# A four-layer graph network on one core: the adjacency loaded once, ScalarE's order in the first stage written by the program, and layer 0's mixing back moved behind the next group's first weight

## The chip, the cores and the metric

The kernel runs on one core of a Trainium2 chip. The metric is the device time of one execution in microseconds (us), the median of several runs. The profile is one more execution, with its own span.

The names used here: TensorE or PE for the matrix engine, VectorE or DVE, ScalarE or ACT, GpSimd or POOL, SyncE or SP. SyncE and ScalarE each have a queue on which the program issues transfers (DMA).

## The reference

The input x has 128 batches of 64 nodes with 256 features; adj is one 64 x 64 matrix for all batches. Four layers follow each other, and each ends in a residual and a layer norm: x = layernorm(x + f(x)).

- Layer 0 is three graph convolutions, relu after the first two: h = relu((adj * adj) (x W1)), with widths 256 to 512, 512 to 1024, 1024 to 256. The weighting is adj * adj elementwise.
- Layer 1 takes the eigenvectors U of the normalized Laplacian of adj, and computes U (relu((U^T x) W1 + b1) W2 + b2).
- Layer 2 is two graph convolutions with adj, then four small LSTMs over windows of 1 to 4 nodes.
- Layer 3 is an attention masked and scaled by adj.

The eigenvectors are computed on the chip too, by Householder steps, bisection and a recurrence, on 64 x 64 tiles. They need adj alone, and layer 1 needs them.

## The kernel before, in words

**Tiling.** The 8192 rows (128 batches x 64 nodes) are 64 tiles of 128 rows; each tile holds two batches, so that a 64 x 64 matrix acts on a tile as a 128 x 128 block-diagonal matrix. All of x stays in one tile X of the on-chip memory. Four tiles (512 rows) are a group; there are 16 groups.

**Two stages.** The first stage runs layer 0 for all groups, and beside it the eigenvectors. The second stage runs layers 1 to 3, three groups at a time. The diff touches the first stage and the loads ahead of it.

**Layer 0 of a group** (`layer0`, line 747). `mixed` multiplies by sqT2, the block-diagonal transpose of adj * adj: it writes transposed products of a block of columns into PSUM, and ScalarE copies them out (m1 from X, m2 from h1). Then come the first weight aw1 (four pairs of 128 x 512 matmuls, each followed by a ScalarE relu into h1, helper `relu`, line 728), the second mixing of h1, the second weight aw2 and the third, aw3. The second weight is done by a Strassen-like scheme: 14 products per group, VectorE sums (ss, tw, the joins into h2), a ScalarE relu of each joined quarter. After the third weight ScalarE copies the result to s3. The mixing back (lines 855 to 862) multiplies s3 by sqT2, two tiles at a time, VectorE adds the result to X, and the layer norm (`scalar_norm`, line 567) is put on the list `norms`: per two tiles two sums, two sums of squares and two final scalings on ScalarE, with a root on GpSimd (lines 578 to 580) between.

**Order.** Two groups are in flight. A loop at the end of the stage (lines 873 to 889) plays the groups as Python generators against a model clock `now`: each matmul adds its cost to it, and a yield says when the group may go on. `between`, called after each matmul, lets the eigenvector generator `eigen` go on when its own time has come; that generator keeps the modelled time at which VectorE is free (`free`) and yields `soon()` or `full(turns)`, a little before or after it. A norm is taken off the list at each of the 14 products (line 835). What is issued in this loop keeps the order of issue on the engines named in `manual_schedule` (line 869): before, TensorE and VectorE. ScalarE's instructions are put in order by the compiler's scheduler, from priorities and its own estimate of times.

**Start.** The adjacency is loaded five times: twice into the diagonal blocks of the zeroed ad2 and once into a64, on ScalarE's queue, and late on SyncE's queue twice into adst, a stack of two copies. The first work of TensorE is the transpose of ad2 (line 871), from which VectorE makes adT2 and sqT2; only then can the first group be mixed. The eigenvectors start from a64 (line 104): degrees, a square root on ScalarE (line 117), scaling matrix dm, and the product with dm on TensorE (line 133), for which the program leaves room with `full(1)`. Each Householder step then has a ScalarE square root (line 174) and one product pc, for which ScalarE writes a half of LV (line 165).

Of the kernel before, what the change touches and what calls it, by code (L numbers as in the profile page):

```python
# [10 lines left out]
F32 = mybir.dt.float32  # L11
AF = mybir.ActivationFunctionType
ALU = mybir.AluOpType
AX = mybir.AxisListType

N = 64
# [39 lines left out]
def eigen(tc, stack, a, ident, cst, u2, ut2, now, free):  # L56
# [9 lines left out]
    nc = tc.nc  # L66
    until = [0.0]
    V, S, PE = Timed(nc.vector, free, until), nc.scalar, nc.tensor
# [5 lines left out]
    def sb(shape, tag):  # L74
        uid[0] += 1
        return wp.tile(shape, F32, tag=tag, name=f"{tag}_{uid[0]}")
# [9 lines left out]
    def soon():  # L86
        return max(free[0], until[0]) - 0.45

    def full(turns=0):
        return max(free[0], until[0]) + 0.3 + 0.6 * turns  # L90
# [23 lines left out]
    dg = sb([N, 1], "c3")  # L114
    V.tensor_scalar(dg, deg, 1e-30, None, op0=ALU.max)
    y = sb([N, 1], "c4")
    S.activation(y, dg, AF.Sqrt)
    V.reciprocal(y, y)
    for _ in range(2):
# [9 lines left out]
    dm = sb([N, N], "dm")  # L129
    V.tensor_scalar(dm, C["eye"], y, None, op0=ALU.mult)  # L130
    pm = ps([N, N], "pa")
    yield full(1)
    mm(pm, m, dm)


# [26 lines left out]
    for i in range(N - 2):  # L162
        j = i + 1
        L = LV[j % 2]
        S.copy(L[:N, 1, :], eye[:, j:j + 1].to_broadcast([N, N]))
        q = sb([N, 16], "q")
        rest, ss, sq, g0, sg, rc, n2, vv, th, s0, c2, qi = (q[:, k:k + 1] for k in range(12))
        u = sb([N, 8], "u")
        v, av, vt, pt, qt = (u[:, k:k + 1] for k in range(5))
        v0 = xr[:, j:j + 1]  # L170
        V.scalar_tensor_tensor(sb([N, N + 1], "junk")[:, j + 1:], xr[:, j + 1:], 1.0, xr[:, j + 1:], op0=ALU.mult,
                               op1=ALU.mult, accum_out=rest)
        V.tensor_scalar(ss, v0, v0, rest, op0=ALU.mult, op1=ALU.add)
        S.activation(sq, ss, AF.Sqrt)
        root = free[0] + 0.6
        yield soon()
        for update in late:
            update()
            yield soon()
        V.tensor_scalar(g0, rest, 1.5e-30, -1.0, op0=ALU.is_gt, op1=ALU.mult)  # L180
        V.tensor_scalar(sg, v0, 0.0, 0.5, op0=ALU.is_ge, op1=ALU.subtract)
        until[0] = root
        yield soon()
        V.reciprocal(rc, sq)
        V.tensor_scalar(n2, ss, rc, sq, op0=ALU.mult, op1=ALU.add)
        V.scalar_tensor_tensor(v0, n2, sg, v0, op0=ALU.mult, op1=ALU.add)
        yield soon()
        V.scalar_tensor_tensor(sb([N, N + 1], "junk")[:, j:N], xr[:, j:N], 1.0, eye[:, j:], op0=ALU.mult,
                               op1=ALU.mult, accum_out=v)
        V.tensor_copy(L[:N, 0, :], v.to_broadcast([N, N]))  # L190
        yield full()
        pq = ps([W, 2, N], "pc")
        mm(pq, L, AQ)
        there, until[0] = until[0], 0.0
        V.tensor_scalar(vv, v0, v0, rest, op0=ALU.mult, op1=ALU.add)
        V.reciprocal(vv, vv)
        V.tensor_mul(th, vv, g0)
        yield soon()
        V.tensor_scalar(s0, v0, th, 2.0, op0=ALU.mult, op1=ALU.mult)
        V.scalar_tensor_tensor(sb([N, N + 1], "junk")[:, j:N], A[:, j:], 1.0, xr[:, j:N], op0=ALU.mult,  # L200
                               op1=ALU.mult, accum_out=av)
        V.tensor_scalar(u[:, 2:4], u[:, 0:2], th, 2.0, op0=ALU.mult, op1=ALU.mult)
        until[0] = there
        yield soon()
        V.scalar_tensor_tensor(sb([N, N + 1], "junk")[:, j:N], pq[:N, 0, j:], th, xr[:, j:N], op0=ALU.mult,
                               op1=ALU.mult, accum_out=c2)
        qr = sb([N, N], "qr")
        V.scalar_tensor_tensor(qr[:, j:], xr[:, j:N], c2, pq[:N, 0, j:], op0=ALU.mult, op1=ALU.add)
        yield soon()
        V.tensor_scalar(qi, qr[:, j:j + 1], th, 2.0, op0=ALU.mult, op1=ALU.mult)  # L210
        nx = xrs[j % 2]
        V.scalar_tensor_tensor(nx[:, j + 1:N], qr[:, j + 1:], s0, pq[N:, 0, j + 1:], op0=ALU.mult, op1=ALU.add)
        V.scalar_tensor_tensor(nx[:, j + 1:N], xr[:, j + 1:N], qi, nx[:, j + 1:N], op0=ALU.mult, op1=ALU.add)
        yield soon()


        def update_a(qt=qt, vt=vt, c2=c2, pt=pt, qr=qr, xr=xr, j=j):
            V.scalar_tensor_tensor(qt, vt, c2, pt, op0=ALU.mult, op1=ALU.add)
            V.scalar_tensor_tensor(A[:, j:], qr[:, j:], vt, A[:, j:], op0=ALU.mult, op1=ALU.add)
            V.scalar_tensor_tensor(A[:, j:], xr[:, j:N], qt, A[:, j:], op0=ALU.mult, op1=ALU.add)  # L220

        def update_q(pq=pq, vt=vt):
            V.scalar_tensor_tensor(QT, pq[:N, 1, :], vt, QT, op0=ALU.mult, op1=ALU.add)

        late = [update_a, update_q]
        xr = nx
# [5 lines left out]
    d, e, ep, g = (de[:, j:j + 1] for j in range(4))  # L232
# [31 lines left out]
    nrm, s1, s1s, s2e, hs = co_[1:6]  # L264
# [18 lines left out]
    lo, h, top, tgt, at, to = co_[14:20]  # L283
# [232 lines left out]
    pt = ps([N, N], "pa")  # L516
# [16 lines left out]
P = 128  # L533
# [62 lines left out]
def kernel(  # L596
# [25 lines left out]
    nc = tc.nc  # L622
    V, S, PE = nc.vector, nc.scalar, nc.tensor
    NT = ROWS // P
    x_t = x.rearrange("b n f -> (b n) f").rearrange("(t p) f -> p t f", p=P)
# [7 lines left out]
    keep = ctx.enter_context(tc.tile_pool(name="keep", bufs=1))  # L633
# [3 lines left out]
    phase_a = ctx.enter_context(ExitStack())  # L637
    wa = phase_a.enter_context(tc.tile_pool(name="wa", bufs=1))
    pa = phase_a.enter_context(tc.tile_pool(name="pa", bufs=1))
    ea = phase_a.enter_context(tc.tile_pool(name="ea", bufs=1))  # L640
# [5 lines left out]
        return t  # L646

    X = keep.tile([P, NT, D], F32, name="X")
    ad2 = keep.tile([P, P], F32, name="ad2")
    nc.gpsimd.memset(ad2, 0.0)  # L650
    adst = keep.tile([P, N], F32, name="adst")
    a64 = ea.tile([N, N], F32, name="a64")
    eig_c = ea.tile([P, len(CONSTS), N], F32, name="eig_c")
    for h in range(2):
        hs = slice(h * N, (h + 1) * N)
        nc.scalar.dma_start(ad2[hs, hs], adj)
    nc.scalar.dma_start(a64, adj)
    for t in range(2):
        nc.sync.dma_start(X[:, t, :], x_t[:, t, :])
    aw1 = load(wa, "aw1", a_w1, "(k p) f -> p k f", [P, 2, 512], p=P)  # L660
    nc.sync.dma_start(X[:, 2:4, :], x_t[:, 2:4, :])
    aw2 = wa.tile([P, 4, 1024], F32, name="aw2")
    for h in range(2):
        cols = slice(h * 512, (h + 1) * 512)
# [2 lines left out]
    for t in range(4, NT, 2):  # L667
        nc.sync.dma_start(X[:, t:t + 2, :], x_t[:, t:t + 2, :])
    nc.sync.dma_start(eig_c, consts)
    for h in range(2):  # L670
        nc.sync.dma_start(adst[h * N:(h + 1) * N, :], adj)

    ident = keep.tile([P, P], F32, name="ident")
    make_identity(nc, ident)
# [1 line left out]
    nc.gpsimd.memset(half, -0.5)  # L676
    ones = keep.tile([P, P], F32, name="ones")
    nc.gpsimd.memset(ones, 1.0)
    adT2 = keep.tile([P, P], F32, name="adT2")
    sqT2 = keep.tile([P, P], F32, name="sqT2")  # L680
    rs_row = keep.tile([P, P], F32, name="rs_row")
    rs_col = keep.tile([P, 1], F32, name="rs_col")
    u2 = keep.tile([P, P], F32, name="u2")
    ut2 = keep.tile([P, P], F32, name="ut2")
# [19 lines left out]
    now = [0.0]  # L704
# [42 lines left out]
    def layer0(g):  # L747
# [97 lines left out]
        for t in (2, 0):  # L845
# [6 lines left out]
                        done["third"] = g  # L852
                    yield now[0]
            S.copy(s3[:, t:t + 2, :], p)
        yield now[0] + 1.5
        for t in (2, 0):
            p = tl(psa, [P, 2, D], "ps", bufs=6)
            mm(p, sqT2, s3[:, t:t + 2, :])
            yield now[0] + 0.4
            x2 = xs[:, t:t + 2, :]  # L860
            VL.tensor_add(x2, p, x2)
            norms.extend(scalar_norm(tc, small, x2, half, spare))

    todo = [layer0(g) for g in range(NT // 4)]
    eig.extend([0.0, eigen(tc, phase_a, a64, ident, eig_c, u2, ut2, now, free)])
    going = []
    with tc.manual_schedule(engines={mybir.EngineType.PE, mybir.EngineType.DVE}):
        pt = tl(psa, [P, 512], "ps", bufs=6)  # L870
        PE.transpose(pt[:, :P], ad2, ident)
        V.tensor_copy(adT2, pt[:, :P])
        V.tensor_mul(sqT2, adT2, adT2)
        while todo or going or eig:
            while todo and len(going) < 2:
                going.append([0.0, todo.pop(0)])
            able = [x for x in going if x[0] <= now[0] + 0.05]
            if able:
                pick = able[0]
            else:  # L880
                pick = min(going + ([eig] if eig else []), key=lambda x: x[0])
                now[0] = max(now[0], pick[0])
            between()
            if pick is eig:
                continue
            try:
                pick[0] = next(pick[1])
            except StopIteration:
                going.remove(pick)
# [1 line left out]
    pr = tl(psa, [P, 512], "ps", bufs=6)  # L891
    PE.matmul(pr[:, :P], ones, adT2, start=True, stop=True)
    V.tensor_copy(rs_row, pr[:, :P])
    V.tensor_reduce(rs_col, ad2, AX.X, ALU.add)
    V.tensor_scalar(wide["c_b0"], wide["c_b0"], rs_col, None, op0=ALU.mult)
    V.tensor_add(cbi, cbi, cbh)
    phase_a.close()
# [354 lines left out]
```

## Time and profile before

| | before |
|---|---|
| median of 3 runs | 2570.01 us |
| lowest, highest | 2565.66, 2570.18 us |
| span of the profiled execution | 2566.4 us |
| its mean granted clock of TensorE | 0.994 of full |
| first mixing by sqT2 starts | 8.0 us |
| first stage ends (first product by u2, layer 1) | 876 us |

How to read the views: the page gives the busy time of each engine, in which matmuls that wait in the array's pipeline count as busy. The view of waits says who waited for whom, in all, how often, and the longest. A row of the timeline is: start, length, engine, line, operation, output <- inputs, shape, count, and in brackets the idle time before it and what ended it. "L51" is a recording helper through which all of the eigenvector code's VectorE work goes; "L719" is that of nearly all matmuls. One matmul of the program is two instructions in the profile (32-bit data).

### The profile page before, as it was taken

How to read it: one execution, taken by the hardware profiler on the slowest of the kernel's cores; microseconds unless marked ns; L12 is line 12 of the kernel's file. 1: busy time of each engine (PE TensorE's matmuls, PEld its weight loads, DVE VectorE, ACT ScalarE, POOL GpSimd, SP SyncE). 2: the span in 40 equal slices, each digit the busy share in tenths (PEclk: the TensorE clock that was granted, in tenths of full speed). 3: DMA queues.
4: the chain of work that ended last, by engine and by line, in shares of the span. 5: the costliest groups of instructions: out<-in, count | busy, mean ns of one | idle time of the engine just before them, and what ended most of it. 6: DMA issues, size and time to landing. Idle time of an engine off the chain costs nothing.

```text
span 2566.4 us, 39034 instructions
## 1 busy us (share of the span) xinstructions
PE 2502.8 (98%) x15020; PEld 2193.7 (85%) x15020; DVE 1414.7 (55%) x5001; ACT 1120.2 (44%) x2727; POOL 133.3 (5%) x316
## 2 busy tenths in 40 slices
PE   8999999999999999999999999999999999999996
PEld 7788887888877889889989889899898898978995
DVE  6877777778884433444453544534435445353235
ACT  3343333433333344544444454444444545445444
POOL 0000000000000100000000000000000000000001
PEclk9999999999999999999999999999999999999998
DMA  6000000000000300000000000000000000000000
GB/s 218 1 1 1 1 1 1 1 1 1 1 1 1 115 1 1 9 9 1 9 6 4 9 1 9 9 1 9 4 6 9 1 9 9 1 9 1 1 1 25
DMA packets 24811, 32.15 MB, mean 13 GB/s; under 512 B 2352, under 2 KB 21552, under 8 KB 24624
## 3 DMA queue, kind: packets, MB, share of 16 engines
q1 hardware_dynamic: 24384, 29.60, 3.4%
q8 instruction: 118, 1.93, 0.3%
q14 instruction: 69, 0.57, 0.1%
q10 hardware_dynamic: 240, 0.05, 0.0%
HBM read 21.25 MB, written 8.39 MB: 12 GB/s over the span
## 4 chain that ended last, share of the span: by engine, by line
PE 81%; DVE 10%; ACT 5%; POOL 2%; issue 1%; DMA 0%; ACTq 0%; POOLq 0%; DVEq 0%
PE ps L719 78%; POOL ln_rs L553 1%; DVE br L51 1%; DVE Q L51 1%; DVE X L563 1%; PE ps L924 1%; ACT gates L1027 1%; DVE ln_st L550 1%; DVE h L51 1%; PE ps L1140 1%; DVE D L51 1%; ACT spare L575 1%; ACT L1027 1%; ACT L1153 1%; DVE X L1090 1%
## 5 line engine op out<-in xcount | busy, mean ns | idle before, releaser
L719 PE MATMUL ps<-w,wih 128*128 128x128 f32 (+2 forms) x4992 | 895.1, 319 | 1.7 <-DVE w L1046 1.7
L719 PEld LDWEIGHTS ps<-w,wih 128*128 128x128 f32 x4992 | 764.5, 191 | 50.9 <-issue 8.4
L1027 ACT ACTIVATE gates<-ps,cbi 128x128 f32<-128x128 f32 (+2 forms) x1248 | 501.7, 409 | 581.9 <-PE ps L719 577.1
L719 PE MATMUL ps<-hs,whh 128*128 128x128 f32 (+2 forms) x3072 | 542.1, 303 | 4.4 <-DVE hs L1037 4.3
L719 PEld LDWEIGHTS ps<-hs,whh 128*128 128x128 f32 x3072 | 453.8, 191 | 33.8 <-issue 11.0
L1032 DVE TENSOR_TENSOR gates<-gates 128x128 f32<-128x128 f32 (+2 forms) x256 | 89.5, 350 | 253.9 <-ACT gates L1027 253.8
L719 PE MATMUL ps<-aw,h 128*128 128x256 f32 x1024 | 227.4, 379 | 0.1
L719 PEld LDWEIGHTS ps<-aw,h 128*128 128x128 f32 x1024 | 192.9, 190 | 26.7 <-ACT h L728 1.2
L728 ACT ACTIVATE h<-h 128x512 f32<-128x512 f32 x128 | 80.8, 631 | 240.3 <-DVE h L51 240.3
L1035 ACT ACTIVATE gates<-c 128x128 f32<-128x128 f32 (+2 forms) x288 | 98.3, 341 | 109.8 <-DVE c L1034 104.0
L1031 DVE TENSOR_TENSOR c<-c,gates 128x128 f32<-128x128 f32 (+2 forms) x192 | 62.5, 325 | 107.7 <-ACT gates L1027 105.3
L719 PE MATMUL ps<-aw,m 128*128 128x512 f32 x256 | 120.9, 593 | 0.0
L719 PE MATMUL ps<-ss,aw 128*128 128x256 f32 x512 | 118.0, 380 | 0.0
L719 PE MATMUL ps<-ss,tw 128*128 128x256 f32 x512 | 118.0, 380 | 0.0
L719 PE MATMUL ps<-m,aw 128*128 128x256 f32 x512 | 117.1, 379 | 0.0
L1046 DVE TENSOR_TENSOR w<-gates 128x256 f32<-128x256 f32 (+2 forms) x160 | 59.4, 377 | 102.3 <-PE ps L719 62.9
L1037 DVE TENSOR_TENSOR hs<-gates 128x128 f32<-128x128 f32 (+2 forms) x192 | 62.8, 328 | 92.6 <-ACT gates L1035 52.8
L563 DVE TENSOR_SCALAR X<-X,ln_mv,ln_rs 128x256 f32<-128x256 f32 x184 | 68.1, 411 | 82.2 <-POOL ln_rs L553 82.2
L719 PEld LDWEIGHTS ps<-m,aw 128*128 128x128 f32 x512 | 96.5, 190 | 18.9 <-issue 5.3
L719 PEld LDWEIGHTS ps<-ss,tw 128*128 128x128 f32 x512 | 96.2, 190 | 13.7 <-issue 1.0
L719 PEld LDWEIGHTS ps<-ss,aw 128*128 128x128 f32 x512 | 96.3, 190 | 12.8
L552 POOL TENSOR_SCALAR ln_rs<-ln_mv 128x2 f32<-128x2 f32 x96 | 23.1, 241 | 1573.0 <-DVE ln_mv L551 1571.2
(294 smaller groups left out, 3142.4 us busy)
## 6 DMA issues: line engine op xcount, KB each, us to landing
out_dram<-X SPq DMA_DIRECT2D x32, 256.0 KB, 2.1
X<-in_x_dram SPq DMA_DIRECT2D x31, 256.0 KB, 6.0
wih<-in_c_ih_dram SPq DMA_DIRECT2D x4, 1024.0 KB, 7.2
aw<-in_a_w_dram SPq DMA_DIRECT2D x3, 1024.0 KB, 9.6
whh<-in_c_hh_dram SPq DMA_DIRECT2D x3, 1024.0 KB, 9.3
aw<-in_a_w_dram SPq DMA_DIRECT2D x1, 512.0 KB, 4.9
cw<-in_c_w_dram SPq DMA_DIRECT2D x2, 256.0 KB, 3.6
X<-in_x_dram SPq DMA_DIRECT2D x2, 128.0 KB, 2.2
```

What stands on the lines that cost most here:

```text
L51: return getattr(self.engine, name)(out, *args, **kw)
L550: nc.vector.bn_stats(st[:, t, :], x[:, t, :])
L553: nc.gpsimd.tensor_tensor(rs, rs, half[:, :n], ALU.pow)
L563: nc.vector.tensor_scalar(x[:, t, :], x[:, t, :], mv[:, t, 0:1], rs[:, t:t + 1], op0=ALU.subtract, op1=ALU.mult)
L719: PE.matmul(out, lhsT, rhs, start=start, stop=stop)
L728: S.activation(dst, src, AF.Relu)
L1027: S.activation(gate[q][:, h, :], pp, AF.Tanh if q == "g" else AF.Sigmoid, bias=bias[:, j:j + 1])
L1031: V.tensor_mul(c[:, h, :], c[:, h, :], gate["f"][:, h, :])
L1032: V.tensor_mul(to, gate["i"][:, h, :], gate["g"][:, h, :])
L1035: S.activation(gate["i"][:, h, :], c[:, h, :] if p > 1 else to, AF.Tanh)
L1037: V.tensor_mul(new[:, h, :], gate["o"][:, h, :], gate["i"][:, h, :])
L1046: V.tensor_mul(hT[:, h, slice(first + p - 1, first + nw * p, p), :], gate["o"][:, h, :].rearrange("p (w b) -> p w b", b=8), gate["i"][:, h ...
```

## The change

The diff does four things.

1. The adjacency comes in once, stacked in adst, one half on each queue ahead of everything else; X[:, 2:4] goes to ScalarE's queue. ad2 and a64 are gone: the transpose reads adst and gives 64 x 128, from which two copies fill the diagonal blocks of adT2 (zeroed by GpSimd), and the eigenvectors read the upper half of adst. The purpose is to have the first data sooner.
2. A square root of a constant at the start asks for ScalarE's table before the first data, and `full(4)` leaves more layer-0 matmuls ahead of the product with dm.
3. ScalarE's order in the first stage is now the order of issue, as TensorE's and VectorE's. So that a square root isn't issued too early, a `yield soon()` goes ahead of it in two places.
4. The mixing back waits 6.5 us of the model clock, not 1.5, in all groups but the last. In the built program this puts it behind the next group's four first-weight pairs; before, the two mixings back stood between these pairs. The second mixing of the next group follows it, and in most groups half of the first mixing of the group after stands ahead of that and half behind.

```diff
@@ -114,6 +114,7 @@
     dg = sb([N, 1], "c3")
     V.tensor_scalar(dg, deg, 1e-30, None, op0=ALU.max)
     y = sb([N, 1], "c4")
+    yield soon()
     S.activation(y, dg, AF.Sqrt)
     V.reciprocal(y, y)
     for _ in range(2):
@@ -129,7 +130,7 @@
     dm = sb([N, N], "dm")
     V.tensor_scalar(dm, C["eye"], y, None, op0=ALU.mult)
     pm = ps([N, N], "pa")
-    yield full(1)
+    yield full(4)
     mm(pm, m, dm)
 
 
@@ -171,9 +172,9 @@
         V.scalar_tensor_tensor(sb([N, N + 1], "junk")[:, j + 1:], xr[:, j + 1:], 1.0, xr[:, j + 1:], op0=ALU.mult,
                                op1=ALU.mult, accum_out=rest)
         V.tensor_scalar(ss, v0, v0, rest, op0=ALU.mult, op1=ALU.add)
+        yield soon()
         S.activation(sq, ss, AF.Sqrt)
         root = free[0] + 0.6
-        yield soon()
         for update in late:
             update()
             yield soon()
@@ -646,19 +647,14 @@
         return t
 
     X = keep.tile([P, NT, D], F32, name="X")
-    ad2 = keep.tile([P, P], F32, name="ad2")
-    nc.gpsimd.memset(ad2, 0.0)
     adst = keep.tile([P, N], F32, name="adst")
-    a64 = ea.tile([N, N], F32, name="a64")
     eig_c = ea.tile([P, len(CONSTS), N], F32, name="eig_c")
-    for h in range(2):
-        hs = slice(h * N, (h + 1) * N)
-        nc.scalar.dma_start(ad2[hs, hs], adj)
-    nc.scalar.dma_start(a64, adj)
+    nc.scalar.dma_start(adst[:N, :], adj)
+    nc.sync.dma_start(adst[N:, :], adj)
+    nc.scalar.dma_start(X[:, 2:4, :], x_t[:, 2:4, :])
     for t in range(2):
         nc.sync.dma_start(X[:, t, :], x_t[:, t, :])
     aw1 = load(wa, "aw1", a_w1, "(k p) f -> p k f", [P, 2, 512], p=P)
-    nc.sync.dma_start(X[:, 2:4, :], x_t[:, 2:4, :])
     aw2 = wa.tile([P, 4, 1024], F32, name="aw2")
     for h in range(2):
         cols = slice(h * 512, (h + 1) * 512)
@@ -667,8 +663,6 @@
     for t in range(4, NT, 2):
         nc.sync.dma_start(X[:, t:t + 2, :], x_t[:, t:t + 2, :])
     nc.sync.dma_start(eig_c, consts)
-    for h in range(2):
-        nc.sync.dma_start(adst[h * N:(h + 1) * N, :], adj)
 
     ident = keep.tile([P, P], F32, name="ident")
     make_identity(nc, ident)
@@ -676,7 +670,10 @@
     nc.gpsimd.memset(half, -0.5)
     ones = keep.tile([P, P], F32, name="ones")
     nc.gpsimd.memset(ones, 1.0)
+
+    S.activation(keep.tile([P, 1], F32, name="root"), ones[:, 0:1], AF.Sqrt)
     adT2 = keep.tile([P, P], F32, name="adT2")
+    nc.gpsimd.memset(adT2, 0.0)
     sqT2 = keep.tile([P, P], F32, name="sqT2")
     rs_row = keep.tile([P, P], F32, name="rs_row")
     rs_col = keep.tile([P, 1], F32, name="rs_col")
@@ -852,11 +849,12 @@
                         done["third"] = g
                     yield now[0]
             S.copy(s3[:, t:t + 2, :], p)
-        yield now[0] + 1.5
+
+        yield now[0] + (1.5 if g == NT // 4 - 1 else 6.5)
         for t in (2, 0):
             p = tl(psa, [P, 2, D], "ps", bufs=6)
             mm(p, sqT2, s3[:, t:t + 2, :])
-            yield now[0] + 0.4
+            yield now[0]
             x2 = xs[:, t:t + 2, :]
             VL.tensor_add(x2, p, x2)
             norms.extend(scalar_norm(tc, small, x2, half, spare))
@@ -864,12 +862,14 @@
 
 
     todo = [layer0(g) for g in range(NT // 4)]
-    eig.extend([0.0, eigen(tc, phase_a, a64, ident, eig_c, u2, ut2, now, free)])
+    eig.extend([0.0, eigen(tc, phase_a, adst[:N, :], ident, eig_c, u2, ut2, now, free)])
     going = []
-    with tc.manual_schedule(engines={mybir.EngineType.PE, mybir.EngineType.DVE}):
+    with tc.manual_schedule(engines={mybir.EngineType.PE, mybir.EngineType.DVE, mybir.EngineType.Activation}):
         pt = tl(psa, [P, 512], "ps", bufs=6)
-        PE.transpose(pt[:, :P], ad2, ident)
-        V.tensor_copy(adT2, pt[:, :P])
+        PE.transpose(pt[:N, :P], adst, ident)
+        for h in range(2):
+            hs = slice(h * N, (h + 1) * N)
+            V.tensor_copy(adT2[hs, hs], pt[:N, hs])
         V.tensor_mul(sqT2, adT2, adT2)
         while todo or going or eig:
             while todo and len(going) < 2:
@@ -891,7 +891,7 @@
     pr = tl(psa, [P, 512], "ps", bufs=6)
     PE.matmul(pr[:, :P], ones, adT2, start=True, stop=True)
     V.tensor_copy(rs_row, pr[:, :P])
-    V.tensor_reduce(rs_col, ad2, AX.X, ALU.add)
+    V.tensor_reduce(rs_col, adst, AX.X, ALU.add)
     V.tensor_scalar(wide["c_b0"], wide["c_b0"], rs_col, None, op0=ALU.mult)
     V.tensor_add(cbi, cbi, cbh)
     phase_a.close()
```

## The prediction

> **What bounds the kernel now.** I read the page first, then the waits of TensorE up to 835 us, then the timeline where those waits lie, then the landing of the first transfers. The page's first part:
>
> ```profile
> PE 2502.8 (98%) x15020; PEld 2193.7 (85%) x15020; DVE 1414.7 (55%) x5001; ACT 1120.2 (44%) x2727; POOL 133.3 (5%) x316
> ```
>
> TensorE (PE) is busy for 2502.8 of 2566.4 us. The diff removes none of its matmuls but a transpose's width, so it can only win back time in which TensorE stood still or ran slowly. The diff ends with the first stage (layer 0 and the eigenvectors): in the built programs all three compute engines have the same rows in the same order from there on. That stage ends at about 876 us. Waits of TensorE in it (what waited, for what: us in all, times, longest):
>
> ```profile
> PE ps L719 <- ACT h L728: 6.9, 5, 2.8
> PE ps L871 <- DMA ad<-in_adj_dram: 6.8, 1, 6.8
> PE pa L93 <- DVE dm L51: 1.5, 1, 1.5
> PE pa L422 <- DVE w L51: 0.6, 1, 0.6
> PE pc L93 <- DVE LV L51: 0.4, 1, 0.4
> ```
>
> Two things matter: the start (adjacency, then dm) and five waits for the relu of layer 0 (L728), all after 600 us. The start in the timeline (start, length, engine, line, operation, idle time before it):
>
> ```profile
> 6.84 0.45 PE L871 MATMUL ps<-ident,ad 128*128 128x128 f32 x1 [6.84 <-DMA ad<-in_adj_dram]
> 8.00 3.41 PE L719 MATMUL ps<-sqT,X 128*128 128x128 f32 x16 [0.71 <-DVE sqT L873]
> 11.52 2.84 PE L719 MATMUL ps<-aw,m 128*128 128x512 f32 x6
> 12.05 1.28 ACT L117 ACT_TABLE_LOAD   x1
> 15.89 0.33 PE L93 MATMUL pa<-dm,m 64*64 64x64 f32 x2 [1.54 <-DVE dm L51]
> 20.77 1.95 PE L719 MATMUL ps<-sqT,X 128*128 128x128 f32 x16
> ```
>
> Nothing useful runs before 8.00, and a table load sits in the chain to dm. The last row, group 1's first mixing, becomes important below. One of the five later waits:
>
> ```profile
> 661.25 0.58 ACT L728 ACTIVATE h<-ps 128x512 f32<-128x512 f32 x1
> 663.04 0.19 POOL L578 TENSOR_SCALAR sn_rs<-sn_va 128x2 f32<-128x2 f32 x1 [46.41 <-ACT spare L575]
> 664.32 1.09 ACT L583 ACTIVATE X<-X,sn_nb,sn_rs 128x256 f32<-128x256 f32 x2 [0.82 <-POOL sn_nb L580]
> 665.32 0.57 ACT L728 ACTIVATE h<-ps 128x512 f32<-128x512 f32 x1
> 665.94 2.27 PE L719 MATMUL ps<-sqT,h 128*128 128x128 f32 x18 [1.25 <-ACT h L728]
> ```
>
> The matmuls whose result the last relu reads were done by about 664.0. But ScalarE (ACT) had the previous group's normalization ahead of it: it stood 0.82 us for GpSimd's root, wrote X twice, and only then did the relu on which TensorE waited.
>
> [...] after the longest wait (772.8 to 775.6) the granted clock was 0.57 in the stretch 775.6 to 779.4. [...] a finished matmul's relu sat behind a norm that waited 0.82 us. [...] In the trace the transfers run at 345 to 390 GB/s from 4 us on[...].
>
> **Part 1, adjacency on two queues.** Before, the third adjacency transfer on ScalarE's queue (issued at 1.92) landed 4.8 us later, 6.7. The first one, issued at 0.72, took 2.4. Both new halves are first on their queues: 0.72 + 2.4 = 3.1 us. From transpose to first mixing it was 8.00 − 6.84 = 1.16 us; two 64x64 copies for one 128x128 add about 0.1. First mixing: 3.1 + 1.26 = 4.4, at most 5.3 if X[:, 2:4] is late; against 8.00 that is 3.6 us sooner. The memset of adT2 comes after 1.6 us on an idle GpSimd, the removed one is covered too, and the later loads of adst (at 34 us) delayed nothing: zero each.
>
> **Part 2, the dm wait.** The start-up Sqrt moves the table load to before the first data, and the program now has five pairs of layer-0 matmuls ahead of the dm product, not three. In the old times, 11.52 + 10 x 0.43 = 15.8, and dm came at 15.84; less most of the 1.28 us load it comes at about 14.8. So the wait goes: from 11.52 + 16 matmuls x 0.43 = 18.4 plus 0.5 for the three small products, group 1's mixing would come at 18.9, not 20.77: 1.8 us saved.
>
> Added: 3.6 + 1.8 = 5.4 us, which would put that mixing at 15.4. But its X must have landed. X[:, 4:6] was issued at 4.99 and landed 11.7 us later (16.7), X[:, 6:8] at 9.22 and 8.3 us later: 17.5. These rest on bandwidth: about 4.3 MB stand ahead of them. The total hardly changes; moving X[:, 2:4] to the other queue only fills the hole at 3 to 4 us (90 GB/s), worth about 0.5 us. The third product of the mixing reads X[:, 6:8]; it ran at 20.77 + 4 x 0.11 = 21.2 and will run at about 17.0. **A new wait of about 1.6 us at this DMA takes the place of the adjacency's; the start is worth 21.2 − 17.0 = 4.2 us.** Ends: 3.7 (landing unchanged at 17.5) and 5.7 (DMA never in the way). Work after that mixing follows at the same distance; VectorE's four 1.23 us subtractions also start later behind a Sqrt that waits for the mixing's copy, but S2 and T2 are needed only two products later, 3.4 us.
>
> **Part 3, ScalarE's order and the mixing back.** In the changed program the norms stand between the next group's products, one per product; no norm stands between the four layer-0 relus and the second mixing. There, the two mixings back (0.86 us each) and four products of the next-but-one group (0.9) follow the last first-layer matmul; that covers a relu (0.2 + 0.6 us). So the five waits go. By full-rate start times (0.11 us per 128-column matmul) they are 0.82, 1.42, 0.95, 2.93 and 1.67 us, a little over the view's 6.9 because ends are modelled: 7.8. With the 2.93 goes the half clock after it: the 26 matmuls took 4.71 us, their like 3.17: 1.5. The wait for w (0.6 to 0.8) I count as gone too: VectorE stands 2.7 to 3.7 us in each group for m2, whose copies the same norms delayed, so it gets ahead. Sum 10.1.
>
> What it adds: each product now has a norm of 0.6 us beside a relu or copy of 0.6, in 1.72 us; with Sqrt and LV copies ScalarE is about 70% busy there. Behind a Sqrt or relu that waits for VectorE stand the copies of p1, m2 and s3, and for those VectorE and TensorE wait. Products have six PSUM buffers and m2 has 3.4 us of slack, so most of this is hidden. Not shown by the trace of before: between 0 (62 Sqrts, all in slack; VectorE mostly waits about 1 us per iteration for TensorE) and 19 us (62 x 0.3 us reaching TensorE). I take 1.2 us. The waits for LV (0.4) and u (0.6) stay in it.
>
> **Sum:** −4.2 − 10.1 + 1.2 = −13.1; 2570.0 − 13.1 = 2556.9, say 2557 us.
>
> **Rivals.** *Half of part 3 comes back*: the fixed order of ScalarE makes new waits for copies in some groups, 5 to 7 us in all. For it: every relu there already waits for VectorE (240 us of ScalarE's idle time). Against: that is idle time of an engine 35% busy. −13.1 + 6 gives 2563. *The DMA is not in the way and nothing replaces the rest*: −5.7 − 10.1 − 1 = −17, 2553; against it stands 17.5 us for X[:, 6:8]. *Slower*: ScalarE's order stalls the Householder chain each iteration, 19 us: 2570 − 14 + 19 = 2575. For it: VectorE's order is fixed, so one late Sqrt holds all behind it; in the profile one Sqrt held it 1.15 us. Against: that one stood behind norms in the mixing, where now are none, and TensorE did not wait.
>
> **How the numbers follow.** Forecast 0.72, half back 0.14, all gains 0.08, slower 0.05, and 0.01 elsewhere. The runs of before spread by 4.5 us (2565.7 to 2570.2), so the range is 2552 to 2564: the forecast, most of the second and the third case. Faster by over 0.2% means under 2564.9: 0.88; within 0.2%, 0.07; slower, 0.05.
>
> **What would show it.** Right: the first mixing at 4.3 to 5.3 us; no table load near the dm product; group 1's mixing waiting for X at 16 to 17.5; no waits of TensorE for L725 (the relu's new line) after 600 us and no granted clock near 0.57 there; the A-to-B turn about 13 us sooner; after it the same length as before. Wrong: many short waits of TensorE for the Householder product or for h2 and m2 between 23 and 520 us[...].

## The result, and the profile after

| | before | changed |
|---|---|---|
| median of the first comparison (4 runs each) | 2569.8 us | 2552.39 us |
| lowest, highest | 2565.66, 2570.18 | 2548.97, 2554.55 |
| ratio of the times, 95% interval | | 0.9935 (0.9917 to 0.9952) |
| span of the profiled execution | 2566.4 us | 2547.2 us |
| first mixing by sqT2 starts | 8.00 us | 4.69 us |
| group 1's first mixing starts | 20.77 us | 18.11 us |
| first stage ends (first product by u2) | 876.11 us | 860.87 us |
| second stage (from there to the end) | 1690.3 us | 1686.3 us |

The changed kernel is faster by 17.4 us; the forecast was 13.1. In the profiles the first stage is 15.2 us shorter, and the second stage, which the change doesn't touch, 4.0 us shorter.

The page of the changed kernel, first part:

```profile
PE 2495.1 (98%) x15020; PEld 2190.4 (86%) x15020; DVE 1414.6 (56%) x5002; ACT 1122.8 (44%) x2727; POOL 130.4 (5%) x316
```

Busy time tells little: TensorE's share is 98% in both, and its busy time falls by 7.7 us though almost none of its work is gone, since the same matmuls can count for more: ten of them took 2.73 us in one profile and 1.69 in the other (the second stage, below). All waits of TensorE up to 835 us are in this view (who waits, for whom: us in all, times, longest):

```profile
PE ps L869 <- DMA adst<-in_adj_dram: 3.4, 1, 3.4
PE ps L716 <- DMA X<-in_x_dram: 1.5, 1, 1.5
PE ps L716 <- DVE sqT L873: 0.9, 1, 0.9
PE pa L93 <- DVE u L51: 0.6, 1, 0.6
PE pa L423 <- DVE w L51: 0.3, 1, 0.3
PE ps L716 <- DMA aw<-in_a_w_dram: 0.2, 1, 0.2
```

No relu (L725) and no dm is left in it, and the new wait for X stands where the forecast put it. The start, in the timeline of TensorE (start, length, line, operation, idle time before it):

```profile
3.37 0.40 PE L869 MATMUL ps<-ident,adst 128*64 128x128 f32 x1 [3.37 <-DMA adst<-in_adj_dram]
4.69 3.81 PE L716 MATMUL ps<-sqT,X 128*128 128x128 f32 x16 [0.93 <-DVE sqT L873]
13.30 0.33 PE L93 MATMUL pa<-dm,m 64*64 64x64 f32 x2
16.23 0.38 PE L93 MATMUL pc<-AQ,LV 128*128 128x128 f32 x2
18.11 2.27 PE L716 MATMUL ps<-sqT,X 128*128 128x128 f32 x16 [1.49 <-DMA X<-in_x_dram]
```

The first mixing starts 3.31 us sooner, but group 1's only 2.66 us sooner: X isn't there. X[:, 4:6] landed at 17.98 us and X[:, 6:8] at 18.73; before, it was 16.73 and 17.48. Now the same place in the same group as the wait that the prediction showed (661 to 666 us there), TensorE and ScalarE:

```profile
655.90 1.88 PE L716 MATMUL ps<-s,sqT 128*128 128x512 f32 x4
656.10 0.60 ACT L725 ACTIVATE h<-ps 128x512 f32<-128x512 f32 x1 [1.12 <-PE ps L716]
657.62 1.05 PE L716 MATMUL ps<-sqT,X 128*128 128x128 f32 x8
658.51 3.74 PE L716 MATMUL ps<-sqT,h 128*128 128x128 f32 x32
```

The last relu runs as soon as its matmuls are done (656.10). Between it and the second mixing, which reads it, stand two mixings back and half a mixing of X, and the 32 matmuls run through.

**Where the time went, by program order.** Waits leave out slow stretches. A better account: take TensorE's instructions in the order of each program, give each its full-rate duration (0.43 us for 512 columns, 0.215 for 256, 0.109 for 128, from undisturbed rows), and subtract the running sum from the real start. What is left is the time lost so far; a small drift is in it for every kernel alike.

| lost so far, us | before | changed | difference |
|---|---|---|---|
| first mixing | 7.78 | 4.47 | 3.31 |
| just before group 1's first mixing | 11.50 | 7.08 | 4.42 |
| just after it | 11.65 | 9.31 | 2.34 |
| after 250 us of work | 13.88 | 10.67 | 3.21 |
| after 590 us of work | 17.72 | 14.17 | 3.55 |
| after 747 us | 22.71 | 15.61 | 7.10 |
| after 765 us | 28.40 | 15.88 | 12.52 |
| end of the first stage | 33.74 | 18.50 | 15.24 |

So the start is worth 2.3 us, the middle 1.2, and from 590 us of work on 11.7.

**The second stage.** Most of the last 4.0 us comes in two steps, at the same two waits of TensorE in both kernels. The first, before, then changed:

```profile
1136.79 2.73 PE L719 MATMUL ps<-w,wih 128*128 128x168 f32 x10 [1.68 <-DVE w L1046]
```

```profile
1121.39 1.69 PE L716 MATMUL ps<-w,wih 128*128 128x168 f32 x10 [1.68 <-DVE w L1046]
```

The wait is 1.68 us in both; the ten matmuls after it take 2.73 us in one and 1.69 in the other. The second, before, then changed:

```profile
2276.59 5.41 PE L719 MATMUL ps<-cw,w 128*128 128x256 f32 x16 [2.33 <-DVE w L951]
```

```profile
2259.40 3.72 PE L716 MATMUL ps<-cw,w 128*128 128x256 f32 x16 [2.32 <-DVE w L951]
```

The granted clock (the column after POOL's, 1.00 is full) says why; before:

```profile
1136.00:1139.00 3.00, 2.21 (x9) 2.21 (x10) 0.55 (x2) 2.04 (x5) 0.00 (x0) 0.71 0.00 0
2277.00:2280.00 3.00, 3.00 (x10) 2.38 (x9) 2.33 (x6) 1.17 (x3) 0.00 (x0) 0.55 0.26 87
```

From 1137.28 to 1140.69 and from 2277.32 to 2280.73 the granted clock was 0.50: a half-clock stretch of 3.4 us follows each wait before, and neither wait in the changed kernel's profile. The second cost 5.41 − 3.72 = 1.7 us. Is that the change's doing, or chance? That became the main question for the experiments, beside which part gives what.

### The profile page after: what moved, and what is told of

It is laid out like the page before. It is cut to its first block, busy times and chain, and to the rows that moved or that the text cites. A ratio compares the mean times of both kernels' runs of the same rounds, so it can differ in the third digit from the quotient of the medians.

```text
span 2547.2 us, 38989 instructions
## 1 busy us (share of the span) xinstructions
PE 2495.1 (98%) x15020; PEld 2190.4 (86%) x15020; DVE 1414.6 (56%) x5002; ACT 1122.8 (44%) x2727; POOL 130.4 (5%) x316
## 4 chain that ended last, share of the span: by engine, by line
PE 87%; DVE 6%; ACT 3%; POOL 2%; issue 1%; DMA 1%; SPq 0%; POOLq 0%; ACTq 0%; DVEq 0%
PE ps L716 84%; POOL ln_rs L554 1%; DVE X L564 1%; PE ps L924 1%; ACT gates L1027 1%; DVE D L51 1%; DVE ln_st L551 1%; PE ps L1140 1%; ACT L1027 1%; ACT L1153 1%; DVE X L1090 1%; PE pc L93 1%; DMA X<-in_x_dram 1%; ACT att L1153 0%; DVE gates L1032 0%
## 5 line engine op out<-in xcount | busy, mean ns | idle before, releaser
L725 ACT ACTIVATE h<-h 128x512 f32<-128x512 f32 x128 | 80.6, 629 | 169.4 <-DVE h L51 169.3
L716 PE MATMUL ps<-aw,m 128*128 128x512 f32 x256 | 114.5, 593 | 0.2 <-DMA aw<-in_a_w_dram 0.2
```

The source lines that it names most:

```text
L716: PE.matmul(out, lhsT, rhs, start=start, stop=stop)
L725: S.activation(dst, src, AF.Relu)
```

## The experiments

"Lost" is the account of the table above. "Stretches" are half-clock stretches of 3.4 us between the end of the first stage and 2500 us; one of twice that length counts as two.

**The start alone** (the changed kernel's loads, early square root and full(4); the rest as before):

```diff
-    with tc.manual_schedule(engines={mybir.EngineType.PE, mybir.EngineType.DVE, mybir.EngineType.Activation}):
+    with tc.manual_schedule(engines={mybir.EngineType.PE, mybir.EngineType.DVE}):
...
-        yield now[0] + (1.5 if g == NT // 4 - 1 else 6.5)
+        yield now[0] + 1.5
```

The three yields are also as before.

> The start alone (adjacency in two halves on two queues, table asked for early, full(4)); ScalarE's order and the mixing back as before. Theory (the start's gain is cut by the landing of X for group 1): adjacency lands at 3.4 us, group 1's first mixing waits 1.0 to 2.0 us for X, the first stage ends 2.0 to 2.8 us sooner than before (876.1), about 873.7; the five waits for the relu (6.9 us in the view) stay at 5 to 8. Time 2567.5, ratio 0.9990. Rival (the start is worth the 4.2 us of the forecast or more, and part 3 correspondingly less): turn at 872 or sooner, ratio 0.9984 or lower. Rival (what a later engine order takes back): turn unchanged at 876.

Measured: 2563.92 us, ratio 0.9979 (0.9970 to 0.9987), 12 runs. Its waits up to 850 us hold

```profile
PE ps L715 <- ACT h L724: 6.8, 5, 3.5
PE ps L715 <- DMA X<-in_x_dram: 0.2, 1, 0.2
```

The relu waits are there, as expected. Lost just after group 1's mixing 8.55 (before 11.65): 3.1 us from the start, with a wait for X of only 0.2, though the loads are those of the changed kernel. The first stage ends at 870.65, 5.5 us sooner. By that number, and by the ratio, the first rival (872 or sooner) would hold, but its reason doesn't: only 3.1 us are the start's, and from 590 us of work on this kernel loses 13.9 where the kernel before loses 16.0. Its five relu waits fall differently; that this is the scheduler placing the norms otherwise is likely, but was not separated.

**ScalarE's order alone:**

```diff
     y = sb([N, 1], "c4")
+    yield soon()
     S.activation(y, dg, AF.Sqrt)
...
+        yield soon()
         S.activation(sq, ss, AF.Sqrt)
         root = free[0] + 0.6
-        yield soon()
...
-    with tc.manual_schedule(engines={mybir.EngineType.PE, mybir.EngineType.DVE}):
+    with tc.manual_schedule(engines={mybir.EngineType.PE, mybir.EngineType.DVE, mybir.EngineType.Activation}):
```

> ScalarE's order by the program alone, with the two yields ahead of the square roots; loads and mixing back as before. Theory A (the order is what matters: norms no longer stand ahead of a relu on ScalarE): waits of TensorE for the relu fall from 6.9 us to under 1.5, no half clock near 770 us, first stage ends 10 to 13 us sooner, at 863 to 866; time about 2558, ratio 0.9955. Theory B (the place of the mixing back is what matters: it gives cover between the last first-weight pair and the second mixing): relu waits stay at 5 or more, turn at 872 or later, ratio above 0.998. A square root that waits and holds up copies would show as new waits of TensorE for the Householder product between 23 and 520 us, up to 19 us.

Measured: 2552.06 us, ratio 0.9940 (0.9928 to 0.9953). Waits for the relu: none. First stage 863.38, 12.7 us sooner, as theory A has it; the order is enough by itself. The time came 6 us under the expected 2558, and the first stage accounts for 12.7 of the 17.3 us to the kernel before (2569.38 in this comparison); the rest lies in the second stage, whose program is unchanged. TensorE and ScalarE after the last first-weight pair:

```profile
658.56 1.88 PE L720 MATMUL ps<-aw,m 128*128 128x512 f32 x4
660.27 1.95 PE L720 MATMUL ps<-sqT,X 128*128 128x128 f32 x16
660.48 0.60 ACT L729 ACTIVATE h<-ps 128x512 f32<-128x512 f32 x1 [1.98 <-PE ps L720]
662.06 3.74 PE L720 MATMUL ps<-sqT,h 128*128 128x128 f32 x32
668.04 0.41 ACT L576 ACTIVATE spare<-X 128x256 f32<-128x256 f32 x1
```

The mixing back still stands between the pairs, but the first norm comes at 668.04, with the products. The cover between the last pair and the second mixing is 1.8 us, and enough. No wait for a Householder product or a copy appears between 23 and 590 us.

**The mixing back alone:**

```diff
-        yield now[0] + 1.5
+
+        yield now[0] + (1.5 if g == NT // 4 - 1 else 6.5)
...
-            yield now[0] + 0.4
+            yield now[0]
```

> The mixing back behind the next group's first weight alone; ScalarE is still put in order by the compiler's scheduler, loads as before. Theory A (order): norms may still be placed ahead of the relus, so over half of the 6.9 us of relu waits stay (3.5 or more) and the turn comes less than 7 us sooner, after 869. Theory B (place of the mixing): relu waits under 1.5 us, turn at 863 to 866, ratio 0.9955.

Measured: 2556.82 us, ratio 0.9952 (0.9938 to 0.9966). Waits for the relu: none here either; first stage 864.80, 11.3 us sooner. Theory A, that the order is needed, falls; both edits do it, each by itself:

```profile
658.40 1.88 PE L719 MATMUL ps<-s,sqT 128*128 128x512 f32 x4
658.60 0.60 ACT L728 ACTIVATE h<-ps 128x512 f32<-128x512 f32 x1 [1.12 <-PE ps L719]
660.18 0.42 ACT L575 ACTIVATE spare<-X 128x256 f32<-128x256 f32 x1 [0.99 <-DVE X L51]
661.00 3.74 PE L719 MATMUL ps<-sqT,h 128*128 128x128 f32 x32
```

A norm needs X from the mixing back. When that comes behind the last pair, the norm's data (660.18, it waits for VectorE's X) isn't there when the relu runs (658.60). In this build the scheduler didn't put it ahead.

**Both, with the start of before** (the last two diffs together):

> ScalarE's order and the mixing back together, with the loads and the start of before. If the parts add up (the start is worth 2.4 us, these two 12.9 of the 15.2 us by which the first stage of the changed kernel is shorter): turn at 863.2, plus or minus 1; no waits for the relu. If they don't add (the later start had been absorbed by waits further on): turn at 861 to 862, as in the changed kernel. Time 2555 to 2558, ratio about 0.995. In all four runs the second stage is the same program: where its length differs from 1690.3 (before) or 1686.3 us (changed), half-clock stretches of about 3.4 us after the same waits of 1.7 and 2.3 us are expected to make the difference, 1.7 us each, and not to follow the edit.

Measured: 2554.49 us, ratio 0.9944 (0.9931 to 0.9956); first stage 863.09 (expected 863.2). Lost from 590 us of work to the end of the stage: 4.35 with both, 4.2 with the order alone, 5.8 with the mixing alone, 16.0 before. So the start and these two add up, as expected, but the order and the mixing don't add to each other: they take away the same waits.

**The changed kernel once more,** unedited:

> The changed kernel itself, unedited, executed again. Theory (the 4 us by which its second stage was shorter in the profile than before's are not the change's): the first stage ends at 860.9 plus or minus 1; the second stage again takes anything between 1686 and 1692 us, and its length goes with the number of half-clock stretches of 3.4 us in it before 2500 us (0 in the first profile of the changed kernel, 2 in that of the kernel before), 1.7 us each. Runs with the same mean granted clock differ from those of before by 15 to 16 us. Median 2552 to 2554. Rival (the change makes the second stage shorter): no half-clock stretch between 861 and 2500 us in this profile either, second stage 1686.

Measured: 2552.04 us, ratio 0.9934 (0.9921 to 0.9946). The first stage ends at 860.71. The second takes 1690.2 us this time, with two stretches, after the same two waits as before. The first of them:

```profile
1121.23 2.85 PE L716 MATMUL ps<-w,wih 128*128 128x168 f32 x10 [1.68 <-DVE w L1046]
```

The same program, the same wait of 1.68 us: 2.85 us here, 1.69 in its first profile. The rival falls. Among executions with the same mean granted clock, 0.996, it took 2549.14 us against 2564.92 to 2565.30 before: 15.8 to 16.2, at the upper end of what was expected.

**Group 1's rows loaded ahead of the second weight:**

```diff
+    for t in range(4, 8, 2):
+        nc.sync.dma_start(X[:, t:t + 2, :], x_t[:, t:t + 2, :])
     aw2 = wa.tile([P, 4, 1024], F32, name="aw2")
...
-    for t in range(4, NT, 2):
+    for t in range(8, NT, 2):
```

> The changed kernel with X[:, 4:8], group 1's rows, loaded ahead of aw2 and aw3 instead of behind them. Theory (the landing of X took half of the start's gain): group 1's first mixing no longer waits (1.49 us before) and starts at 16.5 to 16.9 us, not 18.1; aw2 lands 0.5 MB later, under 1.6 us, and is needed only at 23 to 25 us, so it makes no wait. First stage ends 1.4 to 1.8 us sooner than in the changed kernel, at 859.2. Rival (aw1 or aw2 becomes the wait): group 0's first product by aw2 waits and the turn stays at 860.9.

Measured: 2554.06 us, ratio 0.9942 (0.9929 to 0.9954); first stage 861.03. Group 1's mixing starts at 17.49 without a wait, later than expected, since group 0 now waited for its own X (1.4 us) and the dm product came at 14.33, not 13.30. At 47 us comes a wait that wasn't foreseen:

```profile
PE ps L718 <- DMA X<-in_x_dram: 1.7, 2, 1.4
PE pc L93 <- DVE LV L51: 0.9, 1, 0.9
```

A Householder product there holds TensorE for 0.9 us; dm had started that chain 1.0 us later. Nothing is won: lost after 40 us of work, 9.57 against 9.40. The end of the first stage stays where the rival has it, but not for the rival's reason: no product waits for the second weight.

**Without part 2:**

```diff
-    S.activation(keep.tile([P, 1], F32, name="root"), ones[:, 0:1], AF.Sqrt)
...
-    yield full(4)
+    yield full(1)
     mm(pm, m, dm)
```

> The changed kernel without part 2: no square root at the start to ask for the table, full(1) in place of full(4). The wait for dm comes back with 1.2 to 2.0 us. Theory (the landing of X for group 1 sets that mixing's start, and part 2 is hidden behind it): the mixing starts at 18.1 as before and the first stage ends at 860.9 plus or minus 0.5. Rival (part 2 is worth the 1.8 us the forecast gave it): the first stage ends at 862.4 or later.

Measured: 2552.98 us, ratio 0.9939 (0.9925 to 0.9952); first stage 860.73, group 1's mixing at 18.22. The wait for dm is back (1.4 us), the one for X is gone, and the sum is the same. But X[:, 6:8] landed at 17.72 here, 1.0 us sooner than in the changed kernel's profile, so the two don't differ in part 2 alone. A profile with part 2 in which it landed as soon (17.45, the run with filler in the tail, below) started group 1's mixing at 16.83, yet a Householder product at 46.6 us then waited 0.65; after 40 us of work it had lost only 0.2 us less than this one. So part 2 is worth next to nothing here, whichever of the two, X or the Householder chain, hides it.

**Filler in three waits of the second stage** (2.3 us, 1.2 and 1.4 us; the wait of 1.68 us is not among them; the results of the fillers are overwritten by the real products):

```diff
                 yield ready[t // 2]
+                for i in range(fill):
+                    PE.matmul(ps[0][:, t * P:(t + 1) * P], ident, rhs, start=True, stop=True)
...
+                if g == 14 and t == j == 0:
+                    for i in range(4):
+                        PE.matmul(p[:, 0, :], ident, cw0[:, 0, :], start=True, stop=True)
                 run(p[:, j, :], [(a[:, k, (t + j) * P:(t + j + 1) * P], cw0[:, k, :]) for k in range(2)])
...
-        a = yield from mixed(g1, adT2, ready)
+        a = yield from mixed(g1, adT2, ready, 4 if g == 0 else 0)
```

> The changed kernel with filler in three waits of the second stage: 4 matmuls of 128 x 256 (1.7 us, their result overwritten by the real product that follows into the same PSUM tile) ahead of group 14's first product by cw0, where TensorE stood 2.3 us for w, and twice 4 of 128 x 128 (0.9 us) ahead of group 0's products by adT2 that stood 1.2 and 1.4 us. Theory [...]: no half clock at those two places in any execution, 1 stretch or none in the second stage before 2500 us, fastest and median runs closer together, median 1 to 2 us below the changed kernel's of the same call. Rival (the fillers delay the real products, because the wait was shorter than they are, or the half clock comes anyway): second stage not shorter than 1688, median the same or 1 us later.

Measured: 2549.69 us (2548.20 to 2549.83), ratio 0.9928 (0.9915 to 0.9940). In its profile no stretch, second stage 1687.3. The median is 2.35 us below the changed kernel's of the same comparison (expected 1 to 2), and the five runs lie within 1.6 us (there 4.1). One profile can't show that no execution has a stretch; and the changed kernel had none in its first profile either, without filler.

**The same filler in the kernel before:**

> The kernel before with the three fillers in the second stage that the changed kernel had in its own run with fillers; nothing of the change in it. If the change's own effect is what the first stage shows (15.2 to 15.4 us) and the rest of the difference of the medians was the draw of half-clock stretches, the two kernels with fillers differ by 15 to 16 us: this one 2565 to 2566 against 2549.7, with a spread between its runs of under 3 us. Rival (the change also shortens the second stage): a difference of 17 us or more, 2567 or later.

Measured: 2563.93 us (2562.64 to 2565.47, 21 runs), ratio 0.9984 (0.9978 to 0.9991). No stretch in the second stage (1685.6 us), the one at 775 us in the first stage still there. With filler the two kernels differ by 2563.93 − 2549.69 = 14.2 us, a little under the 15 to 16 expected, not over it. They ran in different comparisons; each against the kernel before of its own, they stand at −4.75 and −19.48, 14.7 apart. The rival falls. In this profile the adjacency landed sooner, and the first stage, whose program is that of before, ended at 875.3, not 876.1.

**Filler in the tail too** (on the changed kernel with filler):

```diff
                 yield ready[t // 2]
+                if g == 15 and first == 2:
+                    for i in range(11):
+                        PE.matmul(ps[0][:, :D], ident, cw0[:, 0, :], start=True, stop=True)
...
         p = ps4()[:, :nt * P]
+        if ending and first == 0:
+            for i in range(18 - g):
+                PE.matmul(p, ident, cw0[:, 0, :], start=True, stop=True)
```

> The changed kernel with the fillers of the run before and, in the tail, 4 and 3 filler matmuls of 128 x 256 ahead of the transposes of the attention in groups 14 and 15 (waits of 2.4 and 1.8 us) and 11 of them (4.7 us) in the wait of 5.3 us for group 15's X. Theory (each of these waits costs a half-clock stretch after it, and the tail's four are on the path to the end): no half clock between 2510 and 2540 while matmuls of the network run; group 15's four products by dw take 3.6 us in place of 6.0 and its last products 1.9 in place of 3.5; together 3 to 5 us, median 2545 to 2547. Rival (the tail's end is set by VectorE and ScalarE, so that faster matmuls there only wait longer, or the clock falls in spite of the filler): median 2549 to 2550, as with the first fillers alone.

Measured: 2546.28 us (2545.63 to 2547.34), ratio 0.9919 (0.9905 to 0.9932), mean granted clock 0.999. The tail with the first fillers only, then with all of them:

```profile
2523.17 1.09 PE L924 MATMUL ps<-ident,X 128*128 128x128 f32 x4 [5.33 <-DVE X L564]
2524.04 6.00 PE L716 MATMUL ps<-w,dw 128*128 128x256 f32 x16
2535.41 3.54 PE L716 MATMUL ps<-w,v 128*128 128x256 f32 x8
```

```profile
2516.81 4.91 PE L1118 MATMUL ps<-cw,ident 128*128 128x256 f32 x22
2522.94 1.89 PE L716 MATMUL ps<-w,dw 128*128 128x256 f32 x8
2525.27 1.99 PE L716 MATMUL ps<-w,dw 128*128 128x256 f32 x8 [0.44 <-ACT w L1122]
2532.63 1.99 PE L716 MATMUL ps<-w,v 128*128 128x256 f32 x8
```

The products by dw take 2 × 1.9 us with 0.44 of waiting between, in place of 6.00, the last ones 1.99 in place of 3.54. This version beats both kernels: its slowest run, 2547.34, is under the fastest of the changed kernel, 2548.63.

**What all ten profiles and the two at the start say on the second stage.** Its program is the same in all that have no filler.

| profile | stretches | second stage, us |
|---|---|---|
| changed, first profile | 0 | 1686.3 |
| before with filler | 0 | 1685.6 |
| changed with filler | 0 | 1687.3 |
| order and mixing | 1 | 1687.8 |
| order alone | 2 | 1689.3 |
| mixing alone | 2 | 1690.0 |
| changed, again | 2 | 1690.2 |
| before | 2 | 1690.3 |
| without part 2 | 2 | 1690.5 |
| group 1's rows early | 3 | 1691.3 |
| the start alone | 3 | 1691.8 |

(With filler in the tail: none, 1683.8.) One stretch costs about 1.7 us, whatever the edit. They don't always lie at the two waits above: with the start alone, the order alone and group 1's rows early, one or two lie between 890 and 905 us, near waits of 1.2 and 1.4 us.

## Why the prediction came out as it did

The direction and the range held, the range by 0.4 us and with some luck: 2552.39 is just above its lower edge, and two of the four runs lie below. The size, 13.1 forecast against 15.2 in the first stage and 17.4 in the medians, was put together from terms of which one was too large, one too small, one of the wrong sign and one missing.

1. **The first mixing sooner (part 1): right.** Forecast 4.4 us and 3.6 sooner; measured 4.69 and 3.31. The later half of the adjacency landed at 3.27, not 3.1, and from transpose to mixing it took 1.32 us (3.37 to 4.69), not 1.26, of which 0.1 was an estimate for the second copy. The start of the kernel before itself scatters: in the five profiles with its loads the first mixing began between 7.04 and 8.00 us, in the seven with the changed loads between 4.69 and 5.00.
2. **The wait for dm goes (part 2): right, but worth nothing by itself.** It is gone, and 4.4 us had been won before group 1's mixing (4.42 in the table, forecast 5.4). Without part 2 the first stage ends at the same time (860.73 and 860.71).
3. **A new wait for X in place of the old one: right as a mechanism, mis-sized.** The forecast's "about 1.6 us" is a slip: it sets the landing for the third product (17.0) against the start of the first (15.4), while its own sum, 5.4 − 4.2, leaves 1.2. Measured was anything from none to 1.5 us in the waits of the runs with these loads and part 2. The step that failed is the landing: "moving X[:, 2:4] to the other queue only fills the hole at 3 to 4 us, worth about 0.5 us", and so the third product at about 17.0. X[:, 6:8] landed at 18.73, 1.25 us later than before and not 0.5 sooner, and the third product started at 18.77. In the first 24 us 7.39 MB were moved after, 7.58 before: the bulk came no sooner. From 4.2 us on the transfers ran at 328 to 406 GB/s before (the forecast had 345 to 390) and at 201 to 406 after. So the start gave 2.34 us where the forecast had 4.2, outside its own ends of 3.7 to 5.7. In the profile with the same loads and the old order it gave 3.1. A second step failed with it: "work after that mixing follows at the same distance". Where X[:, 6:8] landed at 17.45, in the profile with filler in the tail, group 1's mixing started at 16.83, but the Householder product at 46.6 us then waited 0.65, and after 40 us of work only 0.4 us was left of the 1.3 by which X had come sooner. X, dm and that product stand close behind each other, and each takes the place of another.
4. **The five relu waits and what hangs on them (part 3): right, mis-sized.** Forecast 10.1; from 590 us of work on, the difference of the time lost is 16.0 − 4.3 = 11.7. By the account, the five waits with the half clock behind one of them come to 10.1 (forecast 7.8 + 1.5), the wait for w to 0.6 (0.8); about 0.9 more was lost before at the stage's last products, which the forecast didn't count. The mechanism, norms ahead of a relu on ScalarE, is shown by two experiments that remove it in two ways. The forecast ascribed the gain to the order and the mixing back together, with "that covers a relu"; the runs show that either is enough, and that the extra cover is not needed.
5. **What ScalarE's fixed order adds: wrong sign.** Taken as 1.2 us lost (0 to 19). No loss shows: between 20 and 590 us of work the changed kernel gains 3.55 − 2.34 = 1.2 us, 0.9 of it between 66 and 250 us, where the kernel before loses 1.99, the changed one 1.09, the order alone 1.13 and the mixing alone 1.09. The single wait for LV (0.4 us) that the waits show there is part of it; the rest isn't named by any view. As the mixing alone, with ScalarE's order left to the scheduler, gains as much, the fixed order isn't the only way to it.
6. **"After it the same length as before": this is where the profile's 4 us went unforeseen.** The forecast counted one half-clock stretch, behind the 2.9 us wait at 772.8, and took the second stage for constant. The profile of before had two more, at 1137 and 2277 us, behind waits of 1.7 and 2.3 us. They are not the change's gain: the changed kernel has them in its second profile. Whether they come differs between executions of one program.

First-stage terms: 2.3 + 1.2 + 11.7 = 15.2 us, against 4.2 − 1.2 + 10.1 = 13.1. The change's own effect is thus about 15 us: the first stage ended at 876.1 and 875.3 in the two profiles of its old program, and at 860.5 to 860.9 in the four of its new one, 14.5 to 15.6 apart; the medians with filler give 14.2 to 14.7. The 17.4 of the medians holds some 2 us more. Filler lowered the median by 4.75 us before and by 2.35 after. The mean granted clock of each execution, known to three places, allows an estimate: (1 − mean clock) times the span, divided by 1.7 us, gives on average some 8.9 half-clock stretches of 3.4 us per execution before (50 executions) and 7.5 changed (9). One of the 1.4 is the one at 775 us, which the change removes; the other 0.4, about 0.7 us, would be the second stage's. Whether that is chance or has a reason was not separated.

On the rivals: "slower" and "half comes back" had rested on new waits that ScalarE's fixed order would make; in the runs with that order the only ones over 0.2 us between 30 and 600 us are two single waits for LV, of 0.9 us (rows early) and 0.65 (filler in the tail). "All gains" (2553) came near the median by the wrong way: the DMA was in the way (1.49 us of waiting for X).

Each half-clock record of the trace ahead of 2500 us lasts 3.413 us in the kernel before, and the three start whole multiples of that apart (775.46 and 1137.28: 361.8 = 106 × 3.413; 2277.32: 440 × 3.413 after the first); one stretch, with group 1's rows early, took 6.8 us. Counted off in steps of 3.413 us from each profile's own stretches, the steps right ahead of the half clock held 2.62, 1.88 and 2.33 us of TensorE's idle time in the kernel before (1.88 is 55% of a step), about 1.9 ahead of the first stretch without part 2, and about 1.7 with group 1's rows early. A step with about 1.8 us in the changed kernel's first profile and one with 1.68 in the kernel before with filler were not followed by half clock. The forecast had looked for half clock behind the longest wait only (2.93 us); that the shorter waits bring none was its author's assumption, and waits of 1.68 and 2.33 us brought it in the very profile that the forecast used.

## What to carry to other kernels

Where an engine serves two streams, work of the less urgent one that is placed ahead can make waits, as the norms on ScalarE did here (five waits of TensorE for a relu, 6.9 us in the view); either fix the order, or make that data come later, and don't count the two gains twice. When a start is cleared of one wait, cost the next two that are due within the same microsecond before booking the sum. When a stage whose program is unchanged changes its length, compare the rows after its waits and the granted clock before ascribing it to the edit: here waits of 1.7 and 2.3 us cost 1.7 us more in some executions. Matmuls with a throw-away result, put into the one of 2.3 us and two of 1.2 and 1.4 us, took 2.4 us off the median, and 5.8 with the tail's (5.3 when each is set against the kernel before of its own comparison).

## What the runs showed of the hardware that was not expected

- A wait of 1.68 us was followed by a half-clock stretch of 3.4 us in one execution and by none in another of the same program: 2.85 and 1.69 us for the same ten matmuls.
- With the same loads, in the same order, group 1's mixing started 1.3 us apart: at 18.11 us in the changed kernel's first profile, after 1.49 us of waiting for X, and at 16.83 with filler in the tail, without a wait.
- Moving one 256 KB load and half of the adjacency to a second queue did not bring the bulk sooner: 7.39 MB in the first 24 us against 7.58.
